# A graph layer on one core: SyncE fetches one set of 128 edges in 120 row by row, beside ScalarE

## The chip, the core and the metric

The kernel runs on one core of a Trainium2 chip. The core's engines work side by side, each through its own list of instructions in order: TensorE (PE, matmuls), VectorE (DVE), ScalarE (ACT), GpSimd (POOL) and SyncE (SP, which issues DMAs only). They wait for one another on semaphores. The metric is device time in microseconds (us); a time of a kernel is the median of several runs.

## What is computed

`x` holds 50000 nodes of 160 numbers (64 scalars, 32 vectors of three). There are 1650000 edges with a source, a destination (sorted) and four numbers `sh`. The layer, cut to what matters:

```python
ss, vv = s[src], v[src]                      # gather the source node's row, for every edge
dot  = einsum('eui,ei->eu', vv, e1)          # products of the row with the edge's four numbers
out0 = C0 * (ss*e0 @ W1 + dot*INV3 @ W2)
out1 = C1 * (p3 + p4 + p5)                   # W3, W4, W5 likewise
m_agg = segment_sum(concat([out0, out1]), dst)   # add up the edges of each destination
h = concat([m_agg[:, :64] @ Ws * LIN_S, (m_agg[:, 64:] @ Wv) * LIN_V])
x = layernorm(x + (x + relu(h)))
```

Weights and sums are linear, so the kernel first adds up, for every node, the rows of its edges' sources weighted with each of the four numbers, and multiplies by the weights afterwards. Most of its work is therefore a gather of rows of 640 bytes, one for each edge.

## The kernel before

**Units and stages.** A *unit* is 128 edges. Edges that lead from a node to itself are sorted out on the way (a table of packed rows, below), so that some 12522 units of gathered rows are left. Six units (`G`) make a group of 32 destination slots, two groups (`PG`) a *pair*, that is 12 units, and 20 groups (`SG`) a *superblock*: 120 units, 10 pairs (`per`). There are 105 superblocks (`NSC`) and 1044 pairs. The main loop (line 981) goes over the pairs and writes out the instructions of all engines in the order in which they stand; from line 979 on the schedule of SP, PE, DVE and ACT is this order, and nothing reorders it.

**A pair.** `gather` (line 430) takes one of four `xg` tiles and issues, on POOL, one indirect DMA a unit (line 437): 128 rows of `x` land in 128 partitions. `spread` (line 448) makes the one-hot matrix with the edges' numbers on DVE (`hot`, line 452, and `ha`, line 455). `group_sums` (line 475) adds up on PE, one matmul a unit (line 482), in `ps`. One pair later `turn_sums` (line 493) turns `ps` on DVE (`sums`, line 497) and adds it to `ring` (line 506), where the sums of 512 nodes stand. A gather into an `xg` tile waits until PE has read that tile four pairs before.

**The set that ACT fetches.** In 102 superblocks (all but the first two and the last) one unit is not gathered by POOL. `list_rows` (line 376), called from `place` (line 386), makes a list `line` of 128 byte addresses on DVE (lines 381, 382). `rows_by_scalar` (line 353) queues 128 steps. Each issues on ACT one DMA of one row (line 369) whose address stands in a register; every 32nd step first loads 32 addresses in registers (line 365). The main loop deals the steps evenly over 10 pairs (lines 1002 to 1009), from pair `FBEGIN` = 4 of the superblock before to pair 4 of the superblock itself, and the unit is used `FWAIT` = 4 pairs later: at spot 96 of 120, the first unit of pair 8. The rows land in one of two `xf` tiles; PE waits for their semaphore ahead of the matmul (line 481).

**What SP issues, in the order of the program.** Per superblock the edges' numbers (`load`, line 260: `r`, `fd`), three pairs ahead of the superblock; per two blocks of 128 nodes the residual rows `xt` (line 744, three buffers), the own rows `xr` and `sa` (line 777) and the finished rows `out<-o` (line 899), which waits for DVE's normalization (line 202). Then the packed rows: the edge list is packed in 11 parts on DVE (`pack`, line 564, with long chains of predicated copies, lines 660 to 667), and each part is stored by SP as single rows (`store` and `put`, lines 694 and 718): an edge row of 27.8 KB and a row of 0.8 KB in turn, each with an address from a register. These stores stand over some 25 pairs of each part. ACT also computes the square roots of the normalization (line 196), and SP's `xt` must have landed before the DVE step `hot` of the pair that needs it (`lands`, line 444).

Of the kernel before, what the change touches and what calls it, by code (L numbers as in the profile page):

```python
# [39 lines left out]
F32 = mybir.dt.float32  # L40
I32 = mybir.dt.int32
BF16 = mybir.dt.bfloat16
U8 = mybir.dt.uint8
# [7 lines left out]
P = 128  # L51
# [26 lines left out]
KM = WS - 1  # L78
REST = 15
LEAD = 3  # L80
NF = 1
FB_ = 2
FBEGIN, FWAIT = 4, 4

def plan(n_nodes, n_edges):
# [24 lines left out]
def tile_gnn_resnorm(ctx: ExitStack, tc: tile.TileContext, x, src, dst, attr, W1, W2, W3, W4, W5, Ws, Wv, out, n_edges):  # L110
# [123 lines left out]
    with tc.tile_pool(name="once", bufs=1) as once, tc.tile_pool(name="raw", bufs=2) as rawp, \  # L234
            tc.tile_pool(name="idx", bufs=2) as idxp, tc.tile_pool(name="rows", bufs=4) as rowp, \
            tc.tile_pool(name="hot", bufs=1) as hotp, tc.tile_pool(name="ops", bufs=3) as op, \
            tc.tile_pool(name="sums", bufs=2) as sump, tc.tile_pool(name="ring", bufs=2) as ringp, tc.tile_pool(name="node", bufs=2) as np_, \
            tc.tile_pool(name="ahead", bufs=3) as aheadp, tc.tile_pool(name="outs", bufs=2) as outp, \
            tc.tile_pool(name="psC", bufs=1, space=PSUM) as psC, tc.tile_pool(name="psK", bufs=2, space=PSUM) as psK, \
            tc.tile_pool(name="psP", bufs=1, space=PSUM) as psP, tc.tile_pool(name="psA", bufs=2, space=PSUM) as psA, \  # L240
            tc.tile_pool(name="psM", bufs=2, space=PSUM) as psM, ExitStack() as later_pools:

        spotp, ownp, fetchp, listp, heldp = (
            later_pools.enter_context(tc.tile_pool(name=name, bufs=bufs))
            for name, bufs in (("spot", 3), ("own", 2), ("fetched", FB_), ("list", 2), ("held", 1)))
        extremes = once.tile([P, 2, NSC], F32, name="extremes")
        count_ = once.tile([1, SG], F32, name="count")
        nc.gpsimd.iota(count_, pattern=[[1, SG]], base=0, channel_multiplier=0, allow_small_or_imprecise_dtypes=True)
# [97 lines left out]
                                                        skip_runtime_bounds_check_because="held within bounds")  # L346
            return spot_of.pop(g)

        fetched, fetches, asked, turns = {}, deque(), [], [0]
        landed = [tc.alloc_semaphore(f"landed{i}") for i in range(4 * FB_)]  # L350
        spots_in = [math.ceil((FBEGIN + per * (i + 1) / NF + FWAIT - per) * PG * G) for i in range(NF)]

        def rows_by_scalar(s, i, line, u):

            turn, xf = turns[0], []
            turns[0] += 1
            sem = landed[turn % len(landed)]

            def one(q, e):
                if not q and not e:  # L360
                    xf.append(fetchp.tile([P, D], F32, name="xf"))
                    fetched[s, spots_in[i]] = xf[0], turn
                if not e:
                    r = q * W + u // NK
                    _, asked[:] = nc.values_load_multi_w_load_instructions(
                        line[r:r + 1, i * W:(i + 1) * W], engines=[ET.Activation], min_val=0, max_val=(N - 1) * 4 * D,
                        skip_runtime_bounds_check_because="held within bounds")
                p = q * W + e
                row = nc.scalar.dma_start(xf[0].bitcast(U8)[p:p + 1], xbytes[ds(asked[e], 4 * D)].rearrange("(o f) -> o f", o=1))
                row.then_inc(sem, 16)  # L370
                tc.no_tile_sem_insts.add(row.ins.name)
                tc.add_to_no_dep_group(f"rows{turn}", row.ins)

            fetches.extend(partial(one, q, e) for q in range(P // W) for e in range(W))

        def list_rows(s, u0, ef):

            line = listp.tile([P, NF * W], I32, name="line")
            held = heldp.tile([P, NF, W], F32, name="held")
            for i, at in enumerate(spots_in):  # L380
                nc.vector.tensor_scalar(held[:, i], ef[:, 0, (u0 + at) % NK], 0.0, float(N - 1), op0=ALU.max, op1=ALU.min)
            nc.vector.tensor_scalar(line, held.rearrange("p i e -> p (i e)"), float(4 * D), None, op0=ALU.mult)
            for i, at in enumerate(spots_in):
                rows_by_scalar(s, i, line, u0 + at)

        def place(cast_):

# [42 lines left out]
        def gather(s, placed, u, n):  # L430

            xg = rowp.tile([P, PG * G, D], F32, name="xg")
            rows = [fetched.pop((s, u + j), None) for j in range(n)]
            for j in range(n):
                if rows[j] is None:
                    rows[j] = xg[:, j, :], None
                    nc.gpsimd.indirect_dma_start(  # L437
                        out=xg[:, j, :], out_offset=None, in_=x,
                        in_offset=bass.IndirectOffsetOnAxis(ap=placed[0][:, u + j:u + j + 1], axis=0))
            return rows  # L440
# [34 lines left out]
        def group_sums(p, rows, ha):  # L475

            ps = psA.tile([P, PG, D], F32, name="ps")
            fresh("ps")
            for j, (xr, turn) in enumerate(rows):
                if turn is not None:  # L480
                    nc.tensor.wait_ge(landed[turn % len(landed)], 16 * P * (turn // len(landed) + 1))
                mm = nc.tensor.matmul(ps[:, j // G, :], ha[:, j].rearrange("p k w -> p (k w)"), xr,  # L482
                                      start=j % G == 0, stop=j % G == G - 1)
                if turn is not None:
                    tc.declare_no_dep(mm.ins, group=f"rows{turn}", reason="their own semaphore is waited for")
                    tc.declare_fence(mm.ins, group=f"rows{turn}")
                if j % G == 0:
                    wrote("ps", mm)
                else:
                    written["ps"][-1].append(mm.ins)  # L490
                yield ps
# [485 lines left out]
                after_pair(p + d, f, b)  # L977
        at_last.close()
        later_pools.enter_context(tc.manual_schedule(engines={ET.SP, ET.PE, ET.DVE, ET.Activation}))
        turning, left = None, 0  # L980
        for p, (s, g, ng) in enumerate(pairs):
            if (p + LEAD) % per == 0 and (p + LEAD) // per + 1 < NSC or not p:
                ahead_ = (p + LEAD) // per + 1
                end = reach(ahead_)
                assert end <= 0 or rows_stored[0] == NR or end <= row_start(rows_stored[0])[0][0]
                raws[ahead_] = load(ahead_)
            if p % per == 0 and s + 1 < NSC:
                after_pair(p + 1, do_cast, s + 1)
                after_pair(p + 2, do_place, s + 1)
                if s + 2 == NSC:  # L990
                    after_pair(p + 4, examine_all)
                    after_pair(p + 6, read_flags)
            rows = gather(s, placed[s], (g - s * SG) * G, ng * G)
            for j, ps in enumerate(group_sums(p, rows, has.pop(p))):
                if j == 1 and turning:
                    turn_sums(*turning)
                    turning = None
                if j == 3 and p + 1 < len(pairs):
                    s1, g1, ng1 = pairs[p + 1]
                    has[p + 1] = spread(placed[s1], (g1 - s1 * SG) * G, ng1 * G)  # L1000
                work(1.0)
                if p % per == FBEGIN and not j:
                    assert len(fetches) == (P * NF if 0 < s < NSC - 2 else 0), (p, s, NSC, len(fetches), len(tasks))
                    begun_at, left = p, len(fetches)
                if left:
                    keep = math.floor(P * NF * (1 - (p - begun_at + (j + 1) / (ng * G)) / per))
                    while left > keep:
                        fetches.popleft()()
                        left -= 1
                if packs and p >= START:  # L1010
                    when = p + (j + 1) / (ng * G)
                    todo = math.ceil(len(packs[0]) * min(1, (when - began) / max(1, due[0] - began)))
                    for step in packs[0][done:todo]:
                        if step:
                            step()
                    done = max(done, todo)
                    if done == len(packs[0]):
                        packs.pop(0), due.pop(0)
                        done, began = 0, when
            turning = p, ps  # L1020
            if p == START - 2:
                with ExitStack() as behind, tc.tile_pool(name="begin", bufs=1) as beginp:
                    for i in first_ones:
                        behind.enter_context(tc.issue_after(i))
                    weights(beginp, psM)
            if p == START - 1:
                with ExitStack() as behind, tc.tile_pool(name="table", bufs=1) as tablep:
                    for i in first_ones:
                        behind.enter_context(tc.issue_after(i))
                    row_table(tablep)  # L1030
                nc.gpsimd.iota(place_, pattern=[[1, L]], base=1, channel_multiplier=0,
                               allow_small_or_imprecise_dtypes=True)
                packp = later_pools.enter_context(tc.tile_pool(name="pack", bufs=1))
            hand_over(p)
# [162 lines left out]
```

## Time and profile before

| | |
|---|---|
| three runs | 17913.42, 17933.31 and 17938.96 us |
| median | 17933.31 us |
| profiled execution, its own time | 18036.58 us |
| its span | 18034.8 us |
| granted TensorE clock, mean | 0.621 |
| gathers on POOL | 12420 |
| row fetches on ACT | 13056 (102 x 128) |
| DMA engines' busy share | 21.5% by POOL's queue, 5.3% by SP's, 0.3% by ACT's |

How to read it: the profile lists for each engine what it was busy with, in groups by line, and how long it sat idle before each group, with what ended that idle time. Issuing a DMA isn't counted as busy, so SP has no busy time at all and ACT's 1% leaves its row fetches out; how full these two are is seen only in the timeline and in the counts of issues in a window. "SPq" and "ACTq" are the issues of SP and ACT. "issue" as the end of an idle time means that the engine waited for nothing that the profile shows.

### The profile page before, as it was taken

To read this page: it belongs to the slowest core of one execution; us is meant where nothing else is said; L and a number is where in the kernel's file an instruction comes from. 1 tells how busy PE (TensorE), PEld (TensorE's weight loads), DVE (VectorE), ACT (ScalarE), POOL (GpSimd) and SP (SyncE) were. 2 spreads that over 40 slices of the span, in tenths; PEclk is the share of its full clock that TensorE was granted. 3 is DMA by queue.
4 is the path that set the end of the run, shared out by engine and by line. 5 is a ranking of instruction groups with operands and counts; after the bars stand their busy time and mean duration, and the time that the engine had idled before them with its cause. 6 is when DMAs were issued, how large, how long until landed. Compare 5 with 4: busy or idle time off the path is not lost.

```text
span 18034.8 us, 122135 instructions
## 1 busy us (share of the span) xinstructions
PE 7025.2 (39%) x28971; PEld 6194.0 (34%) x28972; DVE 7589.3 (42%) x12430; ACT 172.2 (1%) x273; POOL 11796.2 (65%) x12433
## 2 busy tenths in 40 slices
PE   3343343334433333333334334333333433333333
PEld 3233333333333333333333333333333333333333
DVE  7344245334524443453345245434533453454233
ACT  0000000000000000000000000000000000000000
POOL 6566666666666666666666666666666666666666
PEclk6666666666666666666666666666666566666666
DMA  2222222222222222222222222222232222222222
GB/s 72 74 72 80 75 73 70 83 75 73 72 82 74 72 81 75 72 70 84 74 73 78 80 70 72 80 74 73 69 86 74 72 74 79 71 73 72 74 70 65
DMA packets 866482, 1343.45 MB, mean 74 GB/s; under 512 B 270014, under 2 KB 637602, under 8 KB 863094
## 3 DMA queue, kind: packets, MB, share of 16 engines
q0 software_dynamic: 596160, 1018.24, 21.5%
q1 hardware_dynamic: 242218, 308.07, 5.3%
q10 hardware_dynamic: 27376, 9.29, 0.3%
q8 instruction: 231, 3.78, 0.1%
q14 instruction: 497, 4.07, 0.1%
HBM read 1263.28 MB, written 71.42 MB: 74 GB/s over the span
## 4 chain that ended last, share of the span: by engine, by line
POOL 33%; issue 32%; PE 13%; another core or an unknown queue 11%; DVE 4%; DMA 3%; DVEq 0%; ACTq 0%; SPq 0%; POOLq 0%; ACT 0%
POOL xg L437 33%; PE ps L482 12%; DMA xg<-in_x,si 3%; PE phb L801 2%; DVE ha L455 1%; DVE ring L506 0%; DVE hot L452 0%; DVE prow L667 0%; DVE pra L667 0%; DVE sums L497 0%; DVE ring L792 0%; DVE pri L662 0%; DVE marks L660 0%; DVE xr L788 0%
## 5 line engine op out<-in xcount | busy, mean ns | idle before, releaser
L437 POOL DMA_INDIRECT xg<-in_x,si x12420 | 11792.7, 949 | 6203.6 <-issue 3640.9
L482 PE MATMUL ps<-xg,ha 128*128 128x160 f32 x24840 | 6390.0, 397 | 9847.6 <-issue 8559.2
L482 PEld LDWEIGHTS ps<-xg,ha 128*128 128x128 f32 x24840 | 5423.2, 267 | 10659.3 <-issue 9304.4
L497 DVE STREAM_TRANSPOSE sums<-ps 128x320 f32<-128x320 f32 x1044 | 530.6, 508 | 8243.2 <-remote 5581.5
L455 DVE TENSOR_TENSOR ha<-hot,pk 128x1536 f32<-128x1536 f32 x1044 | 1830.0, 1753 | 53.8 <-DVE hot L452 12.9
L801 PE MATMUL phb<-BWk,ring 128*128 128x160 f32 (+1 forms) x3910 | 1217.7, 394 | 791.8 <-issue 791.0
L801 PEld LDWEIGHTS phb<-BWk,ring 128*128 128x128 f32 (+1 forms) x3910 | 950.0, 271 | 782.4 <-issue 781.9
L506 DVE TENSOR_TENSOR ring<-ring,sums 128x160 f32 x2087 | 682.2, 327 | 312.5 <-issue 203.7
L186 DVE SCALAR_TENSOR_TENSOR y<-phb,xt 128x320 f32<-128x320 f32 x196 | 95.1, 485 | 1315.9 <-remote 638.9
L452 DVE TENSOR_TENSOR hot<-bank,rel 128x384 f32<-128x384 f32 x1044 | 572.8, 549 | 76.2 <-DMA xt<-in_x 73.2
L667 DVE COPY_PREDICATED prow<-marks,prow 128x2370 f32<-128x2370 int32 (+5 forms) x198 | 549.7, 2776 | 1.1
L792 DVE STREAM_TRANSPOSE ring<-xr 128x1280 f32<-128x1280 f32 x188 | 465.2, 2474 | 7.1 <-DVE xr L788 0.6
L667 DVE COPY_PREDICATED pra<-marks,pra 128x1580 f32<-128x1580 int32 (+5 forms) x198 | 378.0, 1909 | 0.0
L788 DVE TENSOR_TENSOR xr<-xr,bank 128x1280 f32<-128x1280 f32 x188 | 278.9, 1483 | 18.2 <-DVE bank L787 6.4
L196 ACT ACTIVATE rstd<-mv,eps_t 128x2 f32<-128x2 f32 x196 | 58.0, 296 | 16430.7 <-DVE mv L191 9545.5
L482 PE MATMUL ps<-xf,ha 128*128 128x160 f32 x204 | 71.0, 439 | 289.9 <-DVE ha L455 127.6
L482 PEld LDWEIGHTS ps<-xf,ha 128*128 128x128 f32 x204 | 42.8, 256 | 316.6 <-issue 237.9
L503 DVE TENSOR_TENSOR ring<-ring 128x196 f32<-128x196 f32 (+20 forms) x485 | 149.2, 372 | 1.8
L202 DVE TENSOR_SCALAR o<-y,mv,rstd 128x160 f32<-128x160 f32 x391 | 131.5, 377 | 26.9 <-issue 11.1
L664 DVE COPY_PREDICATED_SCALAR hit<-marks,none 128x395 int32 (+5 forms) x198 | 130.0, 656 | 10.1 <-DVE pri L662 3.3
L751 DVE MEMSET ring<- 128x1280 f32 (+1 forms) x98 | 119.3, 1218 | 22.7 <-issue 22.7
L190 DVE BATCH_NORM_STATS2 st<-y 128x6 f32<-128x160 f32 x391 | 121.6, 311 | 6.7
(351 smaller groups left out, 2048.0 us busy)
## 6 DMA issues: line engine op xcount, KB each, us to landing
xf<-in_x ACTq DMA_DIRECT2D x13056, 0.6 KB
xg<-in_x,si POOLq DMA_INDIRECT x12420
xr<-in_x SPq DMA_DIRECT2D x187, 640.0 KB
r<-edges SPq DMA_DIRECT2D x100, 384.0 KB
edges<-prow SPq DMA_DIRECT2D x1330, 27.8 KB
xt<-in_x SPq DMA_DIRECT2D x195, 160.0 KB
out<-o SPq DMA_DIRECT2D x195, 160.0 KB
pra<-in_attr SPq DMA_DIRECT2D x10, 2370.0 KB
```

The lines of the kernel that those rows point to most:

```text
L202: nc.vector.tensor_scalar(o[:n, i], y[:n, i], mv[:n, i, 0:1], rstd[:n, i:i + 1], op0=ALU.subtract, op1=ALU.mult)
L437: nc.gpsimd.indirect_dma_start(out=xg[:, j, :], out_offset=None, in_=x, in_offset=bass.IndirectOffsetOnAxis(ap=placed[0][:, u + j:u + j + ...
L452: idle[:] = [nc.vector.tensor_tensor(hot[:, :n], slotsP[:, 0:W].unsqueeze(1).to_broadcast([P, n, W]), rel[:, u:u + n].unsqueeze(2).to_broa ...
L455: nc.vector.tensor_tensor(ha[:, :n], hot[:, :n].unsqueeze(2).to_broadcast([P, n, NK, W]), pk[:, :, u:u + n].rearrange("p k u -> p u k").un ...
L482: mm = nc.tensor.matmul(ps[:, j // G, :], ha[:, j].rearrange("p k w -> p (k w)"), xr, start=j % G == 0, stop=j % G == G - 1)
L497: nc.vector.transpose(at[:, :ng], ps[:, :ng].rearrange("p g (b f) -> p g b f", f=FB))
L503: nc.vector.tensor_tensor(ring[k][:, b, :past], ring[k][:, b, :past], ring[k - 1][:, b, S:S + past], op=ALU.add)
L506: nc.vector.tensor_tensor(here, here, at[:, i], op=ALU.add)
L667: nc.vector.copy_predicated(what[:n, a:e], mi[:, r].unsqueeze(2).to_broadcast([n, e - a, what.shape[2]]), what[:n, a + d:e + d])
L788: nc.vector.tensor_tensor(xr[:, :nq], xr[:, :nq], sumP[:, :nq].unsqueeze(2).to_broadcast([P, nq, D]), op=ALU.mult)
L792: nc.vector.transpose(ring[k][:, :, c0:c0 + nq * W].rearrange("p b (w q) -> p q b w", q=nq), xr[:, :nq].rearrange("p q (b f) -> p q b f", ...
L801: wrote("misc", nc.tensor.matmul(ph[:nb], ring[k][:, i, c0:c0 + nb], BWk[:, i, :], start=i == 0, stop=i == ND - 1))
```

## The change

ACT's fetch becomes a class `Fetcher`, made twice: for ACT as before, with two tiles (`xscalar`), and for SP, with two tiles of its own (`xsync`) and semaphores of its own. Each takes one unit of 120 in the same 102 superblocks; ACT's at spot 98, SP's at spot 104, both in pair 8. The steps of both are dealt over the same 10 pairs; at each unit ACT's stand ahead of SP's. The list `line` has a column for each, so DVE clips two columns and scales both in one instruction. PE's wait for the rows is now part of the matmul. The pool of `sums` has one buffer, not two. The core of the diff:

```diff
-NF = 1
-FB_ = 2
+BY_SCALAR, BY_SYNC = 1, 1
...
-            tc.tile_pool(name="sums", bufs=2) as sump, ...
+            tc.tile_pool(name="sums", bufs=1) as sump, ...
...
+        class Fetcher:
+            def __init__(self, engine, et, pool, n, place):
...
+                self.landed = [tc.alloc_semaphore(f"{pool.name}{i}") for i in range(4 * (n + 1))]
+                self.spots = [math.ceil((FBEGIN + per * (i + 1) / n + FWAIT - per) * PG * G) + place for i in range(n)]
...
+                def one(q, e):
+                    if not q and not e:
+                        tile_.append(self.pool.tile([P, D], F32, name="x" + self.pool.name))
+                        fetched[s, at] = tile_[0], sem, count, f"{self.pool.name}{turn}"
+                    if not e:
+                        r = q * W + u // NK
+                        _, self.asked = nc.values_load_multi_w_load_instructions(
+                            line[r:r + 1, :], engines=[self.et], min_val=0, max_val=(N - 1) * 4 * D,
+                            skip_runtime_bounds_check_because="held within bounds")
+                    p = q * W + e
+                    row = self.engine.dma_start(tile_[0].bitcast(U8)[p:p + 1],
+                                                xbytes[ds(self.asked[e], 4 * D)].rearrange("(o f) -> o f", o=1))
+                    row.then_inc(sem, 16)
...
+            def deal(self, gone):
+                keep = math.floor(P * self.n * (1 - gone))
+                while self.left > keep:
+                    self.rows.popleft()()
+                    self.left -= 1
...
+        fetchers = [Fetcher(*f) for f in ((nc.scalar, ET.Activation, scalarp, BY_SCALAR, 2), (nc.sync, ET.SP, syncp, BY_SYNC, 8)) if f[3]]
...
-            for j, (xr, turn) in enumerate(rows):
-                if turn is not None:
-                    nc.tensor.wait_ge(landed[turn % len(landed)], 16 * P * (turn // len(landed) + 1))
+            for j, (xr, sem, count, key) in enumerate(rows):
                 mm = nc.tensor.matmul(...)
+                if key:
+                    mm.wait_op(sem, count, "sem-ge")
...
+                for f in fetchers:
+                    if f.left:
+                        f.deal((p - begun_at + (j + 1) / (ng * G)) / per)
```

In the changed kernel the gather stands on line 459, the matmul on 502, the row fetch on 376 and its loads of addresses on 372, and SP's stores on 739.

More of the change, by code (lines that the diff above doesn't have):

```diff
@@ L236, in tile_gnn_resnorm @@
             tc.tile_pool(name="hot", bufs=1) as hotp, tc.tile_pool(name="ops", bufs=3) as op, \
-            tc.tile_pool(name="sums", bufs=2) as sump, tc.tile_pool(name="ring", bufs=2) as ringp, tc.tile_pool(name="node", bufs=2) as np_, \
+            tc.tile_pool(name="sums", bufs=1) as sump, tc.tile_pool(name="ring", bufs=2) as ringp, tc.tile_pool(name="node", bufs=2) as np_, \
             tc.tile_pool(name="ahead", bufs=3) as aheadp, tc.tile_pool(name="outs", bufs=2) as outp, \
@@ L241, in tile_gnn_resnorm @@
             tc.tile_pool(name="psM", bufs=2, space=PSUM) as psM, ExitStack() as later_pools:
-        spotp, ownp, fetchp, listp, heldp = (
+        spotp, ownp, listp, heldp, scalarp, syncp = (
             later_pools.enter_context(tc.tile_pool(name=name, bufs=bufs))
-            for name, bufs in (("spot", 3), ("own", 2), ("fetched", FB_), ("list", 2), ("held", 1)))
+            for name, bufs in (("spot", 3), ("own", 2), ("list", 2), ("held", 1),
+                               ("scalar", BY_SCALAR + 1), ("sync", BY_SYNC + 1)))
         extremes = once.tile([P, 2, NSC], F32, name="extremes")
@@ L347, in find @@
             return spot_of.pop(g)
[L349 to L374, printed above, removed]
@@ new lines, in tile_gnn_resnorm, with prepare, begin @@
+        fetched = {}
+        class Fetcher:
+            def __init__(self, engine, et, pool, n, place):
+                self.engine, self.et, self.pool, self.n = engine, et, pool, n
+                self.rows, self.turn, self.left, self.asked = deque(), 0, 0, []
+                self.landed = [tc.alloc_semaphore(f"{pool.name}{i}") for i in range(4 * (n + 1))]
+                self.spots = [math.ceil((FBEGIN + per * (i + 1) / n + FWAIT - per) * PG * G) + place for i in range(n)]
+                assert all(0 <= at < per * PG * G for at in self.spots)
+            def prepare(self, s, line, at, u):
+                turn, tile_ = self.turn, []
+                self.turn += 1
+                sem, count = self.landed[turn % len(self.landed)], 16 * P * (turn // len(self.landed) + 1)
+                def one(q, e):
[11 more added lines that the diff above has]
+                    row.then_inc(sem, 16)
+                    tc.no_tile_sem_insts.add(row.ins.name)
+                    tc.add_to_no_dep_group(f"{self.pool.name}{turn}", row.ins)
+                self.rows.extend(partial(one, q, e) for q in range(P // W) for e in range(W))
+            def begin(self, wanted):
+                assert len(self.rows) == wanted * self.n * P
+                self.left = len(self.rows)
+            def deal(self, gone):
[3 more added lines that the diff above has]
+                    self.left -= 1
@@ L376, in list_rows @@
+        fetchers = [Fetcher(*f) for f in ((nc.scalar, ET.Activation, scalarp, BY_SCALAR, 2), (nc.sync, ET.SP, syncp, BY_SYNC, 8)) if f[3]]
+        wanted = [(f, at) for f in fetchers for at in f.spots]
+        assert len({at for _, at in wanted}) == len(wanted)
         def list_rows(s, u0, ef):
-            line = listp.tile([P, NF * W], I32, name="line")
-            held = heldp.tile([P, NF, W], F32, name="held")
-            for i, at in enumerate(spots_in):
+            line = listp.tile([P, len(wanted), W], I32, name="line")
+            held = heldp.tile([P, len(wanted), W], F32, name="held")
+            for i, (f, at) in enumerate(wanted):
@@ L381, in list_rows @@
                 nc.vector.tensor_scalar(held[:, i], ef[:, 0, (u0 + at) % NK], 0.0, float(N - 1), op0=ALU.max, op1=ALU.min)
-            nc.vector.tensor_scalar(line, held.rearrange("p i e -> p (i e)"), float(4 * D), None, op0=ALU.mult)
-            for i, at in enumerate(spots_in):
-                rows_by_scalar(s, i, line, u0 + at)
+            nc.vector.tensor_scalar(line, held, float(4 * D), None, op0=ALU.mult)
+            for i, (f, at) in enumerate(wanted):
+                f.prepare(s, line[:, i], at, u0 + at)
@@ L435, in gather @@
                 if rows[j] is None:
-                    rows[j] = xg[:, j, :], None
+                    rows[j] = xg[:, j, :], None, None, None
                     nc.gpsimd.indirect_dma_start(
@@ L478, in group_sums @@
             fresh("ps")
-            for j, (xr, turn) in enumerate(rows):
-                if turn is not None:
-                    nc.tensor.wait_ge(landed[turn % len(landed)], 16 * P * (turn // len(landed) + 1))
+            for j, (xr, sem, count, key) in enumerate(rows):
                 mm = nc.tensor.matmul(ps[:, j // G, :], ha[:, j].rearrange("p k w -> p (k w)"), xr,
                                       start=j % G == 0, stop=j % G == G - 1)
-                if turn is not None:
-                    tc.declare_no_dep(mm.ins, group=f"rows{turn}", reason="their own semaphore is waited for")
-                    tc.declare_fence(mm.ins, group=f"rows{turn}")
+                if key:
+                    mm.wait_op(sem, count, "sem-ge")
+                    tc.declare_no_dep(mm.ins, group=key, reason="their own semaphore is waited for")
+                    tc.declare_fence(mm.ins, group=key)
                 if j % G == 0:
@@ L979, in tile_gnn_resnorm @@
         later_pools.enter_context(tc.manual_schedule(engines={ET.SP, ET.PE, ET.DVE, ET.Activation}))
-        turning, left = None, 0
+        turning = None
         for p, (s, g, ng) in enumerate(pairs):
@@ L1002, in tile_gnn_resnorm @@
                 if p % per == FBEGIN and not j:
[L1003 to L1009, printed above, removed]
+                    begun_at = p
+                    for f in fetchers:
+                        f.begin(0 < s < NSC - 2)
+                for f in fetchers:
+                    if f.left:
+                        f.deal((p - begun_at + (j + 1) / (ng * G)) / per)
                 if packs and p >= START:
```

## The prediction

> **What bounds the kernel now.** I read the page's busy times first, then what ended POOL's idle time, then one stretch of the timeline on PE, SP and ACT. The columns of the group row are line, engine, operation, tile, count | busy us, mean ns | idle before; those of the wait rows are us in total, times, longest.
>
> ```profile
> PE 7025.2 (39%) x28971; PEld 6194.0 (34%) x28972; DVE 7589.3 (42%) x12430; ACT 172.2 (1%) x273; POOL 11796.2 (65%) x12433
> L437 POOL DMA_INDIRECT xg<-in_x,si x12420 | 11792.7, 949 | 6203.6 <-issue 3640.9
> ```
> ```profile
> POOL xg L437 <- issue: 3640.9, 11834, 6.3
> POOL xg L437 <- remote: 1402.0, 315, 6.8
> POOL xg L437 <- PE ps L482: 1100.6, 216, 55.3
> ```
>
> POOL does one thing: 12420 gathers of 128 rows. Each takes 0.949 us, and 11834 of them follow the last one at 3640.9 / 11834 = 0.31 us. Run without a stop they would need 12420 x 1.26 = 15.6 ms of the span's 18034.8 us. The other 2.5 ms are 531 stalls (the two rows below, 1402.0 + 1100.6 us), 4.7 us each: a gather needs a buffer that PE has not emptied. So POOL is the first bound, and PE's lateness is the second. Why is PE late, when it is busy for 39%?
>
> ```profile
> 9026.83 0.30 PE L482 MATMUL ps<-xg,ha 128*128 128x160 f32 x1 [1.10 <-issue]
> 9029.63 0.42 PE L482 MATMUL ps<-xg,ha 128*128 128x160 f32 x1 [2.50 <-issue]
> 9031.06 0.43 PE L482 MATMUL ps<-xg,ha 128*128 128x160 f32 x1 [1.01 <-issue]
> ```
> ```profile
> 2076.64 0.70 SPq L718 DMA_DIRECT2D edges<-prow  x1
> 2079.45 0.70 SPq L718 DMA_DIRECT2D selves<-mine  x1
> 2081.54 0.00 SPq L718 DMA_DIRECT2D edges<-prow  x1
> 2081.56 0.21 SPq L718 DMA_DIRECT2D selves<-mine  x1
> 2081.87 0.23 SPq L718 DMA_DIRECT2D edges<-prow  x1
> 2082.19 0.23 SPq L718 DMA_DIRECT2D selves<-mine  x1
> ```
> ```profile
> 1978.92 81.62 ACTq L369 DMA_DIRECT2D xf<-in_x  x62
> 9031.94 28.05 ACTq L369 DMA_DIRECT2D xf<-in_x  x29
> ```
>
> The reader is to see that PE, SP and ACT share stretches in which each issues an instruction only every 0.7 us or more. At 9026 PE starts a matmul every 1.4 us or more and waits for nothing that the profile shows ("issue"). SP issues a DMA each 2.1 to 2.8 us until 2081.5, and then one each 0.32 us. ACT's row by row fetch took (81.62 + 28.05) / 91 = 1.205 us a row over these two bursts, both rates mixed. I don't know the cause; what I use is the price that it puts on each DMA issued by ACT or SP while POOL gathers. It ends when POOL stops:
>
> ```profile
> 768.02 0.94 POOL L437 DMA_INDIRECT xg<-in_x,si  x1 [55.27 <-PE ps L482]
> ```
> ```profile
> edges<-prow SPq DMA_DIRECT2D x44, 27.8 KB
> selves<-mine SPq DMA_DIRECT2D x44, 0.8 KB
> xt<-in_x SPq DMA_DIRECT2D x1, 160.0 KB
> ```
>
> The issue rows are those of 717 to 768 us, inside POOL's pause of 55.27 us: 89 DMAs on SP in 51 us, 0.57 us each, half of them of 27.8 KB. And this pause is itself a precedent, as the page's row for the one-hot step shows:
>
> ```profile
> L452 DVE TENSOR_TENSOR hot<-bank,rel 128x384 f32<-128x384 f32 x1044 | 572.8, 549 | 76.2 <-DMA xt<-in_x 73.2
> ```
>
> DVE waited 73.2 us for one load that stood in SP's queue behind stores, so the whole kernel waited for SP.
>
> **How full SP is.** SP's busy time isn't on the page, since issuing isn't counted. So I take one of the stages in which SP stores the packed rows (1743 to 2158 us: waits, then issues, then both windows of the same length, with and without stores):
>
> ```profile
> SPq L718 <- DMA edges<-prow: 6.8, 9, 1.0
> ```
> ```profile
> xg<-in_x,si POOLq DMA_INDIRECT x286
> edges<-prow SPq DMA_DIRECT2D x117, 27.8 KB
> selves<-mine SPq DMA_DIRECT2D x117, 0.8 KB
> edges<-prow SPq DMA_DIRECT2D x8, 1.1 KB
> selves<-mine SPq DMA_DIRECT2D x8, 0.4 KB
> ```
> ```profile
> 1743.00:2158.00 415.00, 159.67 (x682) 141.00 (x682) 119.78 (x220) 1.48 (x5) 271.13 (x286) 0.63 0.27 76
> 2300.00:2715.00 415.00, 167.62 (x666) 147.43 (x666) 189.25 (x317) 2.47 (x7) 273.78 (x289) 0.62 0.26 69
> ```
> ```profile
> L718 SPq DMA_DIRECT2D edges<-prow x1414: 1/277/7990, 473.0 to 16841.5; - x177
> L718 SPq DMA_DIRECT2D selves<-mine x1411: 2/314/2021, 475.1 to 16840.8; - x177
> ```
> ```profile
> 9048.25 0.38 SPq L899 DMA_DIRECT2D out<-o  x1
> ...
> 9050.96 8.76 SPq L777 DMA_DIRECT2D sa<-selves  x1
> 9148.64 0.38 SPq L899 DMA_DIRECT2D out<-o  x1
> ...
> 9150.27 1.24 SPq L744 DMA_DIRECT2D xt<-in_x  x1
> 9234.45 0.38 SPq L899 DMA_DIRECT2D out<-o  x1
> ```
>
> In 415 us SP issued 250 stores (117 + 117 + 8 + 8), and its longest kind of wait in them came to 6.8 us: SP had no slack there. That is 1.66 us a store with the loads between them, 1.52 us a DMA with the 23 loads and sends of the same window counted. The whole run has 1414 + 1411 = 2825 stores, so 2825 x 1.66 = 4690 us of SP. Outside these stages SP issues two short bursts in 186.2 us (9048.25 to 9234.45), 11.5 and 2.9 us long, so 14.3 / 186.2 of the other 13345 us, 1025 us. SP is used for 5715 us and free for 12320.
>
> **The change part by part.**
>
> Removed: 102 gathers on POOL (one spot of 120 in 102 of 105 superblocks, as ACT has them). In the two windows above 575 gathers took 830 us, 1.443 us each with their share of the stalls; 102 x 1.443 = 147 us. Without that share it would be 102 x 1.26 = 129; I take 147, since a shorter list stalls less often too.
>
> Added on SP: 102 x 128 = 13056 row fetches, each a register move and a DMA, and 408 loads of 32 addresses. No row shows a single-row fetch on SP. The bounds: 0.97 us a row (ACT's better burst, 28.05 / 29) and 1.52 (SP's own DMAs beside stores). I take 1.205, ACT's two bursts together: the same instruction with the same address loads, from an engine that also issues between POOL's gathers. SP then needs 13056 x 1.205 = 15732 us and has 12320 - 147 = 12173. That holds 10102 rows; 2954 are left over.
>
> What the left-over rows cost: SP is a queue in order, so they delay the stores, the loads of the next superblock's edges, xt, and the rows themselves. PE's matmul at spot 104 now waits for a semaphore of the 128 rows; behind it on PE stand all later matmuls, DVE waits for their sums, and POOL for the buffers, four pairs later. Then POOL stops, and with it the low rate, so SP works off the rest at the price of the pause. That is 0.32 us a row (2081.87 to 2082.19) up to the 0.57 us of the pause; a load of 32 addresses (row below, median 2202 ns) adds 0.07 to the row. I take 0.40, as what is late is mostly rows: 2954 x 0.40 = 1182 us.
>
> ```profile
> L365 ACTq TENSOR_LOAD <-line x408: 4/2202/3080, 289.7 to 17854.5; - x136
> L381 DVE TENSOR_SCALAR held<-r x99: 167/180/378, 881.1 to 17717.8; 128x32 f32<-128x32 f32 x99
> ```
>
> The small parts, each at nothing: one more clip on DVE per superblock (180 ns, 102 times, 18 us if DVE's 58% idle time did not cover it); the sums tile with one buffer instead of two (writer and readers are both DVE and follow each other, so no new wait; without that cover at most one extra semaphore wait in 1044 pairs); ACT's spot at 98 instead of 96 (two matmuls later); the semaphore wait inside the matmul instead of ahead of it (102 instructions of PE less). Bytes don't count: a set is 82 KB whoever fetches it.
>
> Sum: 18035 - 147 + 1182 = 19070 us of span. The profiled execution took 18036.58 us against the median of 17933.31, 103 us more; taking that off gives **18970 us**, 5.8% slower. With 0.97 a row 506 rows are left: 18035 - 147 + 202 - 103 = 17990. With 1.52 it is 5047 rows, 2019 us, 19800; and 20660 if these also cost 0.57.
>
> **A rule weighed.** The trace's row first: SP's 250 stores filled 415 us. The Trainium skill, page "DMA: Bandwidth & Descriptors", section "Issuing engines are not separate DMA queues", says that several issuing engines save only the time to initiate a transfer, which is usually small beside the transfer. By that sentence the rows would cost SP little and the sum would end with the gathers saved, 17786 us; the first rival is that outcome, and the stores' row speaks against it.
>
> **The rivals.**
> 1. *SP keeps up*, and the gathers' 147 us come back whole: 17933 - 147 = 17786. It needs a row at 0.96 us or less on SP (then at most 367 rows are left, and 367 x 0.40 eats the 147). For it: ACT does carry one set now, and SP is free for 68% of the span. Against it: ACT's two bursts, 0.97 and 1.32, both lie above.
> 2. *SP keeps up, but its issues slow the rest*: the window with 250 stores has 3 gathers fewer in 415 us, 4.3 / 250 = 0.017 us an issue. 13056 x 0.017 = 227 us, so 17933 - 147 + 227 = 18013. It turns slower from 0.0113 us an issue on. Against it as the main effect: the fill of SP above.
> 3. *ACT falls behind too*, since SP's issues take turns with ACT's, and ACT now spends 128 x 1.205 = 154 of some 172 us a superblock on its set: above 19800.
>
> **How the numbers follow.** The forecast (SP overloaded, 18100 to 19800) gets 0.65, rival 1 0.14, rival 2 0.12, rival 3 0.09. The range 17950 to 19800 takes in the forecast with its prices from 0.97 to 1.52 and rival 2; rival 1 and rival 3 stay out. A measurement of this kernel can tell about 0.2% from no change. Faster by more: 0.14 (rival 1). Within: 0.04, the edge between rivals 1 and 2. Slower: 0.82.
>
> **What the changed profile would show.** 12318 gathers on L459, still 0.95 us each. SP issuing rows in long runs at about 1.2 us a row; its waits for o gone. New pauses of POOL of tens of us, ended by PE at L502, with PE waiting for SP's rows or DVE for xt or r; most in the stages with stores, where both want SP (some 105 stores and 128 rows in a superblock of 172 us). Between the pauses the gathers' pace stays near 1.44 us. Wrong would be: SP still waiting for o most of the time and POOL's stalls as before (rival 1), or no long pauses and all of the time in more short stalls (rival 2).

## The result and the profile after

The changed kernel took **19645.89 us** (median of 4 runs, 19610.03 to 19693.0) against 17927.6 for the kernel before (4 runs, 17913.42 to 17938.96): a ratio of **1.096, 95% interval 1.0934 to 1.0987**. The forecast was 18970, so the direction was right and the loss came out at 1718 us instead of 1037.

One thing must be known for all that follows. Runs came in groups, each with runs of the kernel before among them. In the recorded group and in one later group the kernel before took 17.93 ms; in four other groups the same program took 15.59 to 15.63 ms, and the changed kernel, repeated in one of these four, took 0.6% less than the kernel before. So each time below is set against the kernel before of its own group, and I call the two the **17.9 ms setting** and the **15.6 ms setting**. The prediction and the recorded result belong to the 17.9 ms setting.

The profiled execution of the changed kernel took 19693.0 us (span 19691.2). First the page: busy times, and groups (line, engine, operation, tile, count | busy us, mean ns | idle before, what ended it).

```profile
PE 6668.8 (34%) x28971; PEld 6010.1 (31%) x28972; DVE 7609.6 (39%) x12532; ACT 172.1 (1%) x273; POOL 11674.5 (59%) x12331
...
L459 POOL DMA_INDIRECT xg<-in_x,si x12318 | 11671.0, 947 | 7982.7 <-issue 3563.8
...
L807 DVE TENSOR_TENSOR sa<-sa,bank 128x32 f32<-128x32 f32 x188 | 34.1, 181 | 3442.2 <-DMA sa<-selves 2717.3
...
L474 DVE TENSOR_TENSOR hot<-bank,rel 128x384 f32<-128x384 f32 x1044 | 572.5, 548 | 486.1 <-DMA xt<-in_x 452.1
...
L502 PE MATMUL ps<-xsync,ha 128*128 128x160 f32 x204 | 64.2, 402 | 498.2 <-DMA xsync<-in_x 452.0
```

A gather still takes 0.95 us, and there are 102 fewer. POOL's idle time grew from 6203.6 to 7982.7 us. Three groups show who is late: DVE waits 2717.3 us for `sa` (before, no wait for that load is listed) and 452.1 us for `xt` (73.2 before), and PE waits 452.0 us for SP's rows. All three tiles are filled by DMAs of SP's queue.

POOL's waits, then SP's (us in total, times, longest):

```profile
POOL xg L459 <- issue: 3563.8, 11656, 1.7
POOL xg L459 <- PE ps L502: 2969.1, 256, 82.9
POOL xg L459 <- remote: 1294.3, 323, 5.7
```
```profile
SPq L555 <- DMA BVd<-BV: 66.4, 1, 66.4
SPq L739 <- DMA edges<-prow: 63.9, 107, 2.0
SPq L372 <- DVE hot L474: 57.8, 9, 49.3
```

The wait for PE at L502 grew from 1100.6 to 2969.1 us, its longest from 55.3 to 82.9. SP's waits show why. Before, its first was 3050.4 us for `o`; now its longest sum is 66.4 us, and the wait for `o` has shrunk to 2.1 us. SP hardly pauses: counted over the trace, its gaps of over 5 us sum to 238 us, where they were 11779. It is full for the whole run.

Here is one of POOL's pauses (9431.9 to 9508.6 us), then SP's queue, first 437 us ahead of the pause and then in it (start, duration or length of the run of equal DMAs, count):

```profile
9508.62 0.94 POOL L459 DMA_INDIRECT xg<-in_x,si  x1 [76.79 <-PE ps L502]
```
```profile
8994.64 30.21 SPq L376 DMA_DIRECT2D xsync<-in_x  x17
...
9442.41 8.02 SPq L376 DMA_DIRECT2D xsync<-in_x  x17
9451.82 0.29 SPq L739 DMA_DIRECT2D edges<-prow  x1
9452.21 0.25 SPq L739 DMA_DIRECT2D selves<-mine  x1
...
9462.70 0.41 SPq L765 DMA_DIRECT2D xt<-in_x  x1
9463.22 2.51 SPq L376 DMA_DIRECT2D xsync<-in_x  x8
...
9478.56 5.01 SPq L798 DMA_DIRECT2D sa<-selves  x1
9483.67 6.79 SPq L376 DMA_DIRECT2D xsync<-in_x  x12
```

While POOL gathers, 17 rows take 30.21 us, 1.78 us each; in the pause 17 take 8.02 and 8 take 2.51 us. Over the whole trace a row took SP 1.27 us between the pauses and 0.40 in them (mean, from one row's register move to the next row's). DVE waits 54.0 us for `sa` in this window; its load stands behind stores and rows in the same queue, as that of `xt` does. The DMAs that SP issued in these 77 us:

```profile
xr<-in_x SPq DMA_DIRECT2D x2, 640.0 KB
xsync<-in_x SPq DMA_DIRECT2D x67, 0.6 KB
edges<-prow SPq DMA_DIRECT2D x34, 27.8 KB
...
selves<-mine SPq DMA_DIRECT2D x34, 0.8 KB
```

Two windows of the same length, the first without stores, the second in a store stage (length, then busy us and count of PE, PEld, DVE, ACT and POOL, the granted clock, DMA share, GB/s):

```profile
8350.00:8520.00 170.00, 65.50 (x261) 59.34 (x261) 80.60 (x129) 0.59 (x2) 111.67 (x119) 0.60 0.26 71
9355.00:9525.00 170.00, 34.85 (x174) 32.68 (x175) 41.82 (x80) 0.59 (x2) 64.20 (x68) 0.59 0.20 56
```

119 gathers in 170 us without stores, 1.43 us each, the pace of before; 68 beside stores. Most of the loss stands in the store stages, though not all: over the whole trace 39 pauses with 1561 us of 2163 lie in the eleven store stages, and 34 shorter ones with 602 us between them.

**Where the time went**, counted over both traces: 73 pauses of POOL of 8 us or more from one gather to the next (4 before), whose time beyond the usual 0.305 us grew by 2036 us; shorter stalls fell by 227 us (PE catches up in a pause, I take it; no run tests that); 102 gathers at 0.949 + 0.305 us are gone, 128 us. 2036 - 227 - 128 = 1681 us, against 1656 between the spans; the other 25 are 12318 gathers that take 2 ns less each.

### The profile page after: what moved, and what is told of

It reads as the page before. It is cut to its first block, busy times and chain, and to the rows that moved or that the text cites. A ratio compares the mean times of both kernels' runs of the same rounds, so it can differ in the third digit from the quotient of the medians.

```text
span 19691.2 us, 148656 instructions
## 1 busy us (share of the span) xinstructions
PE 6668.8 (34%) x28971; PEld 6010.1 (31%) x28972; DVE 7609.6 (39%) x12532; ACT 172.1 (1%) x273; POOL 11674.5 (59%) x12331
## 3 DMA queue, kind: packets, MB, share of 16 engines
q0 software_dynamic: 591264, 1009.88, 19.6%
## 5 line engine op out<-in xcount | busy, mean ns | idle before, releaser
L459 POOL DMA_INDIRECT xg<-in_x,si x12318 | 11671.0, 947 | 7982.7 <-issue 3563.8
L502 PE MATMUL ps<-xg,ha 128*128 128x160 f32 x24636 | 5992.3, 389 | 11394.0 <-issue 10308.0
L502 PEld LDWEIGHTS ps<-xg,ha 128*128 128x128 f32 x24636 | 5193.0, 262 | 12015.2 <-issue 10871.4
L807 DVE TENSOR_TENSOR sa<-sa,bank 128x32 f32<-128x32 f32 x188 | 34.1, 181 | 3442.2 <-DMA sa<-selves 2717.3
L474 DVE TENSOR_TENSOR hot<-bank,rel 128x384 f32<-128x384 f32 x1044 | 572.5, 548 | 486.1 <-DMA xt<-in_x 452.1
L502 PE MATMUL ps<-xsync,ha 128*128 128x160 f32 x204 | 64.2, 402 | 498.2 <-DMA xsync<-in_x 452.0
L502 PEld LDWEIGHTS ps<-xsync,ha 128*128 128x128 f32 x204 | 46.7, 262 | 504.1 <-DMA xsync<-in_x 458.8
```

The source lines that it names most:

```text
L459: nc.gpsimd.indirect_dma_start(out=xg[:, j, :], out_offset=None, in_=x, in_offset=bass.IndirectOffsetOnAxis(ap=placed[0][:, u + j:u + j + ...
L474: idle[:] = [nc.vector.tensor_tensor(hot[:, :n], slotsP[:, 0:W].unsqueeze(1).to_broadcast([P, n, W]), rel[:, u:u + n].unsqueeze(2).to_broa ...
```

## The experiments

**Theory A**, the prediction's: SP issues its DMAs in order at a price, and the store stages no longer fit into its queue beside 128 rows a superblock. **Theory B**: each row fetch slows the rest by itself (rival 2 made larger). **Theory C**: one of the small parts costs the time. Runs of one group share the kernel before. The differences in the 15.6 ms setting are all under 1%; they are read beside the intervals, and none is a large gain. In the edits "..." stands for lines not shown.

### First group: 15.6 ms setting

*The change without SP's rows.*

```
-BY_SCALAR, BY_SYNC = 1, 1
+BY_SCALAR, BY_SYNC = 1, 0
```

> The change with SyncE's fetches switched off: the new class, the wait inside the matmul, one buffer of sums instead of two and spot 98 stay, and all 119 gathers but ScalarE's are GpSimd's as before. Theory A (SyncE's queue is overfull: its DMAs are issued in order, and the stores of a store stage no longer fit beside 128 rows in a superblock) and theory B (every row fetch of SyncE slows the rest by itself, 1865 us over 13056 fetches = 0.14 us each): 17930 us, within 0.2%. Theory C (one of the small parts, which the prediction put at nothing, costs a good part of the 1718 us): 18300 us or more.

Measured: 15586.28 us against 15586.3, ratio 1.0 (0.9991 to 1.0009). The level was not expected; the kernel before had moved with it. By the ratio, the small parts cost nothing, and theory C falls, in this setting. POOL's waits in this trace:

```profile
POOL xg L459 <- issue: 3540.8, 11611, 0.8
POOL xg L459 <- PE ps L502: 197.4, 643, 1.7
```

The 2.5 ms of stalls that the prediction began with aren't there, although POOL's gather takes the same 949 ns. 12420 x 1.254 us, 15575 of the span's 15600.5 us, is nearly all there is.

*One DMA a superblock in place of 128* (which rows they are is left out):

```
+if self.engine is nc.sync:
+    if not q and not e:
+        block = self.engine.dma_start(tile_[0], x[turn * P:(turn + 1) * P, :])
+        block.then_inc(sem, 16)
...
+    return
```

> SyncE brings its 128 rows of each superblock with a single DMA of 128 neighbouring rows of x (which rows they are is left out: the block number takes the place of the indices), so that its 13056 row fetches become 102 DMAs with the same tiles, bytes and waits, and GpSimd gathers 118 of 120 sets as in the changed kernel. Theory A: SyncE is as free as before, only the gain of 102 gathers at 1.443 us is left, 17930 - 147 = 17780 us. Theory B: the same, as the fetches are gone; what bytes or landings alone cost would show as a time above 17780. Theory C: 18300 us or more.

Measured: 15458.2 us, ratio 0.9917 (0.9904 to 0.9931), so 128 us less than the kernel before. That is the gain alone: 102 x 1.254 = 128 us. The gain of this setting is a gather without stalls.

*128 rows at fixed addresses* (the indices, their loads and the register moves are left out):

```
+if self.engine is nc.sync:
+    row = self.engine.dma_start(tile_[0][p:p + 1], x[turn * P + p:turn * P + p + 1, :])
...
+    return
```

> SyncE fetches 128 single rows in each superblock, but at fixed addresses (the indices are left out), so that its loads of addresses and the one register move ahead of each DMA go: one instruction a row instead of two. Theory A, if SyncE pays by instruction (1.2 us a row were two steps of about 0.6 to 0.7 us while GpSimd gathers): about 0.65 us a row, 83 us of a superblock's 171, so that only part of the stores is late: 18000 to 18700 us. Theory A, if it pays by DMA: 1.2 us a row still, about 19600 us. Theory B: as many row fetches as in the changed kernel, 19600 us.

Measured: 15485.97 us, ratio 0.9935 (0.992 to 0.9951). Theory B would have had to lose time on 13056 added fetches and doesn't, in this setting. Whether SP pays by instruction or by DMA while it is held up isn't told: in this trace a row costs 0.295 us (median), against 0.322 with its move, and nothing is scarce.

*Rows only for superblocks without stores.*

```
+WITH_STORES = (2, 3, 9, 10, 11, 12, 19, 20, 21, 28, ...)   # 37 superblocks
...
-f.prepare(s, line[:, i], at, u0 + at)
+if f.engine is not nc.sync or s not in WITH_STORES:
+    f.prepare(s, line[:, i], at, u0 + at)
```

> SyncE fetches a set only for those 65 of 102 superblocks whose span of fetching has no stores of a pack in it; GpSimd gathers the set itself in the other 37. The output is the reference's. Theory A: the pauses of GpSimd, which stand in the store stages, go, and 65 gathers are saved: 17930 - 65 x 1.443 = 17836 us; as 128 rows at 1.23 us and some 12 us of other DMAs take 169 of the 171 us of a superblock, up to 150 us may be left of them: 17830 to 17990. Theory B: 65/102 of the loss, 17930 + 65/102 x 1718 = 19020 us.

Measured: 15512.34 us, ratio 0.9952 (0.9939 to 0.9966): 74 us less, where the saved gathers alone would give 65 x 1.254 = 82.

### Second group: 15.6 ms setting

*64 DMAs of two rows* (every second index is left out):

```
...
+two = 2 if self.engine is nc.sync else 1
+if e % two:
+    return
-row = self.engine.dma_start(tile_[0].bitcast(U8)[p:p + 1],
-                            xbytes[ds(self.asked[e], 4 * D)].rearrange("(o f) -> o f", o=1))
+row = self.engine.dma_start(tile_[0].bitcast(U8)[p:p + two],
+                            xbytes[ds(self.asked[e], two * 4 * D)].rearrange("(o f) -> o f", o=two))
```

> SyncE brings its 128 rows with 64 DMAs of two neighbouring rows each (every second index is left out), all else as in the changed kernel. Theory A: a superblock without stores has 64 x 1.23 + 12 = 91 us of its 171 to do, one with stores is still overfull: per pack 257 stores at about 1.4 us, 165 us of rows and 29 us of the rest over 21 pairs of 17.1 us leave about 195 us late, 127 us beyond the slack of four pairs, issued at 0.42 of the price: 53 us for each of 11 packs, so 17780 + 590 = 18370 us, 18000 to 18700. Theory B: half the loss, 17780 + 933 = 18720 us.

Measured: 15507.94 us (15472.85 to 15512.99) against 15624.53, ratio 0.9927 (0.991 to 0.9943): no loss, like the single DMA and the fixed rows of the first group.

*SP's rows without ACT's:*

```
-BY_SCALAR, BY_SYNC = 1, 1
+BY_SCALAR, BY_SYNC = 0, 1
```

> ScalarE's fetches are switched off and SyncE's kept, so that as many rows are fetched one by one as in the kernel before, and GpSimd gathers 119 sets. Theory A: SyncE is as overfull as in the changed kernel: 19400 to 19900 us. A theory by which it is the sum of both engines' fetches that is too much (26112 where 13056 were well): 17930 us.

Measured: 15638.97 us, ratio 1.0009 (1.0 to 1.0019). Here SP carries its set beside the stores at next to no cost, so this run can't tell its two theories apart.

*Two sets on SP:*

```
-BY_SCALAR, BY_SYNC = 1, 1
+BY_SCALAR, BY_SYNC = 1, 2
```

> SyncE fetches two sets in 120 instead of one, 13056 rows more. Theory A: every one of the added DMAs is left over, and is issued at the price of a pause, 0.33 us for a row alone to 0.56 us as the mean of all that a pause holds, while a saved gather frees 1.443 us: 19650 - 147 + 13056 x 0.36 to 0.56 = 24200 to 26800 us. Theory B: 19650 - 147 + 1865 = 21370 us.

Measured, one run: 15578.55 us, 46 us under the kernel before. Both expectations fail, having been made for the other setting. But the sign of a full queue comes back: 204 gathers at 1.254 us are 256 us, of which most is given back, 172 us of it in 10 pauses of POOL, and DVE waits for the same tile:

```profile
DVE sa L807 <- DMA sa<-selves: 1276.7, 65, 64.1
```

### The changed kernel again: 15.6 ms setting

No edit; the program of the recorded result.

> The changed kernel as it stands, once more, beside the kernel before on the same chip, since in the runs so far the kernel before took 15586 to 15625 us and not 17928. Theory A, with the price of a fetch by SyncE as what decides: where the kernel before takes about 15600 us and a row costs SyncE 0.32 us (as the runs with fewer fetches show there), 13056 rows take 4.2 ms, nothing is left over and the gain of 102 gathers at 1.254 us stands alone: 0.992 of the kernel before, 15460 to 15500 us. Where it takes about 17930 us and a row costs 1.2 us: 1.096, as recorded. Theory B (each fetch slows the rest): about 1.1 in both.

Measured: 15531.65 us against 15625.32, ratio **0.994 (0.9923 to 0.9956)**. The same program that lost 9.6% takes 0.6% less. Its trace against the recorded one: groups, SP's wait, and SP's rows in the timeline.

```profile
L459 POOL DMA_INDIRECT xg<-in_x,si x12318 | 11712.0, 951 | 3795.6 <-issue 3520.6 <-PE ps L502 203.2 <-DMA xg<-in_x,si 59.2
L502 PE MATMUL ps<-xg,ha 128*128 128x160 f32 x24636 | 9633.4, 505 | 5167.4 <-DMA xg<-in_x,si 4658.8 <-issue 285.4 <-DVE ha L477 72.4
```
```profile
SPq L920 <- DVE o L201: 3010.6, 122, 69.1
```
```profile
8999.93 8.08 SPq L376 DMA_DIRECT2D xsync<-in_x  x24
```

24 rows in 8.08 us, 0.34 us each, while POOL gathers (0.38 over the whole trace, as a mean from row to row; the median is 0.32); SP waits for `o` again, so it keeps up. PE waits for the gathers' landing (4658.8 us) and hardly for "issue" (285.4), where the recorded trace has this:

```profile
PE ps L502 <- issue: 10409.3, 2903, 110.2
```

Not all of these 10409.3 us are a slow pace: they take in PE's idle time in the pauses (its gaps of over 20 us at this line sum to 4389 us, whatever ended them, and to 120 here). But PE's gaps of 1.5 to 3 us at this line, which aren't pauses, number 1908 there and 269 here.

That the price of SP's instructions differs can be read from one line of each trace, the register move ahead of a row (duration in ns: min/median/max), recorded first, then this run:

```profile
L376 SPq MOVE xsync<-in_x x13056: 1/29/1647, 289.9 to 19608.4; - x198
```
```profile
L376 SPq MOVE xsync<-in_x x13056: 29/29/39, 244.7 to 15318.1; - x198
```

A move never takes over 39 ns here, and up to 1647 ns there.

### SP's rows made dearer: 17.9 ms setting

The same fetches and bytes, but SP loads its 32 addresses anew before every 4th row, and in a second kernel before every 2nd:

```
-if not e:
+if e % (4 if self.engine is nc.sync else W) == 0:
```

> The changed kernel, in which SyncE loads the same 32 addresses anew before every fourth row (eight loads where there was one), so that a row costs it 0.32 + 2.3 / 4 = 0.89 us where the kernel before takes 15.6 ms and a row 0.32 us; bytes, fetches and waits are the same. Theory A (the price of a row in SyncE's queue decides): 13056 rows come to 11.7 ms, with some 3.4 ms of stores, sends and loads to 15.1 of 15.5 ms, so that the queue is full and the stores are over: per pack 239 us of rows, 139 of stores and 36 of others in a store stage of 313 us, 40 to 100 us late beyond the slack, for 11 packs 15500 + 450 to 1100 = 15950 to 16600 us, with pauses of GpSimd in the store stages as in the recorded profile. Theory B: no more fetches than before, 15530 us. If the kernel before takes 17.9 ms here, a row costs 1.2 us and more by the loads, and theory A gives over 23000 us.

> The same with a load before every second row: 0.32 + 2.3 / 2 = 1.47 us a row. Theory A: 13056 x 1.47 = 19.2 ms and 3.4 ms of the rest; SyncE's queue sets the end of the whole kernel, 22600 us, 21500 to 23500. Theory B: 15530 us.

Measured: 22923.66 us against 17926.22, ratio 1.2788 (1.2744 to 1.2831), and 27298.69, ratio 1.5228 (1.5184 to 1.5272). This group met the 17.9 ms setting. For it the first expectation had "over 23000" by theory A, missed by 0.3%; the second had none. By theory B nothing changes against the recorded 19646, since no fetch was added. POOL's and DVE's waits, for the first kernel and then the second:

```profile
POOL xg L459 <- PE ps L502: 6408.8, 301, 105.3
```
```profile
DVE sa L807 <- DMA sa<-selves: 6830.3, 187, 120.1
```
```profile
POOL xg L459 <- PE ps L502: 10759.9, 320, 139.2
```
```profile
DVE sa L807 <- DMA sa<-selves: 9530.3, 187, 157.2
```

Only loads of registers were added, and only on SP, and POOL's wait for PE went from 2969.1 to 6408.8 and 10759.9 us. The pauses of 8 us or more number 73, 135 and 175 and sum to 2163, 5679 and 10168 us. So the pauses grew by 3516 and 8005 us where the span grew by 3263 and 7614: all of the added time stands in them, and none in a slower pace of the gathers. In this setting SP's queue is what decides. It decides outside the store stages too: of the first kernel's pauses 3109 us of 5679 lie there. The 2856 added loads of the first kernel, at 2.13 us each (median), are 6.1 ms of SP's time, of which 3.3 ms came to the end. I take it that a load issued while POOL gathers pushes rows into a pause, where they are cheaper: in that trace a row took 1.23 us between the pauses and 0.38 in them.

### Two repeats: 15.6 ms setting

No new edits: the kernel with rows only for superblocks without stores, and the one with a single DMA a superblock (which again leaves out which rows they are).

> Once more the kernel in which SyncE fetches only for the 65 superblocks without stores. Where the kernel before takes 17.93 ms (a row costs SyncE 1.2 us): theory A 17836 us with nothing left over, up to 17990 if the full queue between the store stages leaves some late; theory B 17930 + 65/102 x 1718 = 19020 us. Where it takes 15.6 ms: 0.995 as before.

> Once more one DMA of 128 neighbouring rows a superblock in place of SyncE's 128. Where the kernel before takes 17.93 ms: theory A 17928 - 102 x 1.443 = 17780 us. If the bytes or a part of the change beside the row fetches bore the loss: well above 17930 us. Where it takes 15.6 ms: 0.992 as before.

Measured: 15552.49 us, ratio 0.9953 (0.9937 to 0.997), and 15497.26, ratio 0.9918 (0.9901 to 0.9934), against 15625.11. They repeat the first group. What these two give in the 17.9 ms setting, and whether rows kept out of the store stages beat the kernel before there, stays open.

## Why the prediction was right or wrong

- **What bounds**: right for the setting it was made in. The slow pace of PE, SP and ACT while POOL gathers (1.27 us for the two instructions of SP's row) is what makes PE late and SP dear. But I took it for a trait of the kernel, and it isn't: it was absent in four of the five later groups, with the same kernel before. The sum was made for the 17.9 ms setting, and that the recorded runs met it again is luck: in the other one the forecast of 5.8% more would have met 0.6% less.
- **The gain**, 147 us, was too small: in the recorded trace 128 us by the gathers alone, 227 us in fewer short stalls and 25 in shorter gathers, 380 together.
- **The price of a row on SP**, 1.205 us: 1.27 us measured between the pauses. Near. So is the number of rows that fits, 10102 forecast and 10550 found between the pauses, but that has luck in it: stores that fell into the pauses made room for rows.
- **"What the left-over rows cost"** is the step that failed, in size. It had 2954 rows left over at 0.40 us, 1182 us. The trace has 3857 DMAs of SP inside the pauses, at 0.56 us each: 2163 us, 2036 of them new. Counted from the start of each of SP's instructions to the start of the next, the rows among them are 2506 at 0.41 us with their moves, so 0.40 was right for a row. What I left out is that what stands in line with them is left over too: 1161 stores at 0.51 us, 190 loads and sends at 1.1, and 166 loads of registers at 1.7 between them. I had counted all stores into the time while POOL gathers, though I had myself named the store stages as the place of the pauses. The 0.57 us of the one pause in the trace before was the right price, and I kept it for the bound. The span came out 621 us above the forecast 19070: 854 us too little for the pauses, less 233 too little for the gain. So two errors partly cancel in the number, which lies near the upper end of the range.
- **The small parts at nothing**: shown in the 15.6 ms setting (ratio 1.0); in the other not tried.
- **Rival 1**, SP keeps up and the gathers saved come back: its condition was a row at 0.96 us or less. It is what happens in the 15.6 ms setting, at 0.38 us a row, with 94 of 128 us kept. The prediction weighed a rule of the Trainium skill (page "DMA: Bandwidth & Descriptors", section "Issuing engines are not separate DMA queues": the time to initiate a transfer is usually small beside the transfer). What the prediction drew from it, that the rows cost SP little, agrees with that trace and not with the recorded one. The rule's own comparison stays open: a packet of 640 bytes on SP's queue took 32 ns in both traces (median), much less than the issuing of a row, but the time from a row's issue to its landing is in no view here.
- **Rival 2**, the issues slow the rest: between the pauses the pace was 1.43 us a gather, as before, and short stalls fell. Against it in both settings.
- **Rival 3**, ACT falls behind too: no. ACT's gaps of over 5 us sum to 5383 us, more than the 3213 before; 1683 us of them lie in the pauses.
- **Marks in the profile after**: mostly as forecast: long runs of rows, the waits for `o` all but gone, tens of us of pause ended by PE at L502 (42 of the 73 are over 20 us), most of it in the store stages, the pace between them unchanged. But the largest wait behind the pauses wasn't named: the prediction had `xt`, `r` and the rows, and DVE waited 2717.3 us for `sa`, six times as long as for `xt`.

## What to carry to other kernels

An engine whose busy time is near nothing can still be full: count its instructions, take their price from the stretch where they are issued, and see whether it still waits for anything. When work no longer fits into a queue in order, everything behind it is late, so the left-over is counted in all DMAs of that queue and priced by what a pause holds. And a gain worked out from a price should be measured where that price differs: here a change worth 0.6% at 0.38 us a row cost 9.6% at 1.27.

## What the runs showed of the hardware

The same program ran at two levels, 15.6 and 17.93 ms, steady within each group of runs. What differs is the pace at which PE, ACT and SP step through instructions while POOL issues indirect gathers. In the two traces of the changed kernel SP's row took 0.38 us against 1.27 (between the pauses), ACT's row 0.35 against 1.02 (whole run), and PE's gaps of 1.5 to 3 us at L502 number 269 against 1908. What doesn't differ: POOL's gather (951 and 947 ns), and the DMA engines' time for the gathers (25.1% of 15531 us and 19.6% of 19691, 3.9 ms both). In the 17.9 ms setting the pace recovers inside a pause of POOL, some 4 us after its last gather: over the 73 pauses SP stepped through 1.1 instructions in the first us, 2.9 in the third and 4.9 in the fifth. What puts a run into one setting or the other, no view of the profile names, and it stays open. Two candidates fall. The granted TensorE clock was higher in the slower setting (0.619 against 0.574). And the chip alone doesn't decide: the chip that the record numbers 2 gave 15.59 ms in the first group and 17.93 ms beside the dearer rows.
